# A fused block of four layers: factors' weights on two queues, condition's products behind the first flips, held gathers, and a further order of the pieces in steps 2 to 10

## The chip, the core and the metric

The kernel runs on one core of one Trainium2 chip. Its metric is the device time of one execution in microseconds (us). Before the change three executions took 637.67 us in the median (636.52 to 637.96).

## What is computed

The input x has 8 sequences of 256 tokens with 256 channels in fp32. Four layers follow one another, each added to its input: a conditioned attention with a gated MLP, a masked attention whose result is normed and modulated by the condition, a quaternion rotation, and a mixture of 8 experts of which each token takes two.

```python
# L0: conditioned norm, attention (16 heads of 16), gated MLP
g, b = t @ gw.T + gb, t @ bw.T + bb
xn = g * x * rsqrt(mean(x * x) + EPS) + b
x = x + attention(xn(x), Wq, Wk, Wv, Wo)
x = x + (silu(xn(x) @ gate_w.T) * (xn(x) @ hid_w.T)) @ out_w.T
# L1: masked attention, norm, modulation by the condition
out = softmax(where(mask, -inf, q @ k.T * scale)) @ v @ Wo.T
mod = silu(conditioning) @ Wc.T + bc
shift, sc = split(mod, 2)
xn = out / rms(out) * rms_scale * (1 + sc) + shift
# L2: a filter and two quaternion products, linear in x
x_rotated = hamilton(q_left_n, hamilton(x_filtered, q_right_conj))
# L3: router, two of eight experts
gate = (rms_w * norm(x)) @ wg_W + wg_b + (genre_embed @ gg_W + gg_b)
topk_w, topk_i = top_k(softmax(gate), 2)
h1 = relu(x @ W1 + b1); h2 = relu(h1 @ W2 + b2)
out = sum over the two experts of (h2 @ W3 + b3) * topk_w
```

## The kernel before

The eight sequences (number b, two blocks of 128 tokens each) go through the first three layers one behind another and overlap: while TensorE does the MLP of sequence b, the attention of a later one and the second attention of an earlier one are put in between. The order of TensorE, VectorE and ScalarE is the order of the program's text, and the text is driven by hand-written strings of words, `STEPS`, one string for each step. A word takes one piece of a generator: `S` is the scores of the next attention round with its exponential (`scores`, lines L1072 and L1074, or L1115 and L1120 for the second attention, named `LastKeys`), `O` its products with the values and the division (`values` and `divide`, L1085 or L1131 and L1096 to L1104), `W` the outward projection (L1144 or L1302), `p` and `q` the next piece of the projections and MLPs (`others`), `.n1` and `.n2` pieces of a norm, `.r1`, `.r2`, `.rot` and `.last` pieces of the second attention's norm and of the rotation with the router, `.pl` and `.table` pieces that place each token's choices in a table in memory, `.early`, `.e` and `.sure` pieces that set up and run expert tiles whose number is already certain.

Per sequence, `qkv_last` forms the keys, the router's part and the values of the second attention in one bank, `pkvl`: L1027 (16 matmuls of 32 x 64), L1034 (8 of 32 x 64) and L1041 (8 of 32 x 128). In the trace each fp32 matmul shows as two records. Then `project` (L982) makes the queries, `pq_a`.

At the start the first sequence is loaded in halves on SyncE's and ScalarE's queues (L581), `small_in` on ScalarE's (L565), the weights of the norms' factors `aff_w` in two halves on SyncE's (L621), the condition's weights `WcT` on GpSimd's (L565). TensorE multiplies the identity with itself meanwhile (`keep_busy`, L2031, written `unread`). Then come the factors (`paff`, L677), the condition's product (`pmod`, L776), the flips of the first normed sequence (`pt_n`, L964), the condition's product with the router's weights (L778, in the same bank) and the first keys (`pk_a`, L982). VectorE and ScalarE turn the flips into `xT_n` (L974, L972) with the factors `aff`.

The experts are worked in tiles of up to 256 tokens. `experts` runs a list of tiles: `records` reads the tile's entries of the table (L1641, SyncE), `fetch` its expert's weights of 2.18 MB (L1650, SyncE), `gather` its tokens by indirect DMA, 128 at a time, issued by GpSimd (L1659), `flip` transposes them (L1678), `hidden` (L1697) and `give` (L1733, L1749) do the layers and add the result to the output. The early tile runs inside steps 8 and 9, four sure tiles from step 9 on, then the rest. `AHEAD` is 3: of the sure tiles, the first three are gathered before the first is flipped. The order of GpSimd's and SyncE's instructions from step 2 on is the scheduler's, by dependences and text.

In the step texts `.sure` stands once near the end of step 8 and twice in step 9. The first `.sure` before the change reads the records and gathers tiles 0, 1 and 2 (six indirect DMAs):

```python
        for i in range(1, AHEAD + 1):
            if groups == NG:
                up_to(i, "fetch", fetch)
            up_to(i, "gather", gather)
        yield
        up_to(AHEAD, "fetch", fetch)
        yield
        flip(0)
        yield
```

Of the kernel before, what the change touches and what calls it, by code (L numbers as in the profile page):

```python
# [18 lines left out]
C = 64  # L19
# [52 lines left out]

STEPS = {
    2: (
        "p*5 .n1 p .n1 p S O p S W p O .n1 S p O p .n2 W p .n2*2 S .pl .r1*3 p*2 S .r1 p .rot*4 p .rot*3 "
        "p end p*3"
    ),
    3: (
        "O S .n1 p*3 W p .last S O p*2 .last .n1 .n2 S p W .r1 p*2 .r1 p .n1 p S .r1 .pl .n2 p .r1 .rot "
        "p .last O S .last .n2 p*3 .rot*2 end .rot p .rot*2 p*2 .rot p"  # L80
    ),
    4: (
        ".last p O S p .last p W .last p S O .n1 p*2 .n2 .n1 p W .last*3 p .n1 p S .pl .n2 .r1 p*2 .pl "
        ".r1 S .r1 .pl p*2 .r1 .pl p .pl*2 p .pl*2 p .rot p .rot .n2 .rot S .rot .pl O .rot p .rot p*2 "
        ".rot end"
    ),
    5: (
        ".n1*2 .last O .last S p*2 S O .last*2 p*2 .pl W p W .r1 p .r1 p .r1*2 S p*2 O .n2 .rot .n2 "
        ".rot*2 S p .n2 .n1 p S .rot p*6 .rot p .rot*2 p*2 end"
    ),  # L90
    6: (
        "O S p O W .last p*2 S .last .n2 .last*2 p*2 S .last p .last W .n2 .pl*3 .n2 p*3 .early .r1*2 "
        "p*2 .pl .early p .pl .r1 .pl .r1 .pl*2 p S .pl O p .early q p S .rot*6 end p*2 .rot"
    ),
# [5 lines left out]
    ),  # L100
    9: ".r2*4 .sure .last S .sure p O .last p*2 .last*3 W .last*2 p*2",
    10: ".r1*2 p .r1*2 p .rot*7 p .rot p*3 .rot p .rot*4 p*3 .rot .pl*6 p .rot*2 .pl*3",
}


# [428 lines left out]
def block_kernel(ctx: ExitStack, tc: tile.TileContext, a: dict, out: bass.AP):  # L534
# [82 lines left out]
    ggw, wgb_b, ggb_b = part["ggw"][0:C, :], part["wgb"], part["ggb"]  # L617
    aff_w = work.tile([C, 4, D], F32, tag="pe", bufs=3, name="aff_w")
    first_factors, second_factors = slice(0, 2), slice(2, 4)
    for js in (first_factors, second_factors):  # L620
        nc.sync.dma_start(out=aff_w[:, js, :], in_=a["aff_w"][:, js, :])  # L621
    wk0 = load_w(nc.sync, "L0_WkT", D, D, pool_a)
    wq0 = load_w(nc.sync, "L0_WqT", D, D, pool_a)
    xs_in[1] = load_x(1)
# [144 lines left out]
    def set_up_condition(cond_g):  # L769

        all3 = ps_s.tile([P, 4 * 2 * S], F32, tag="s", name="pmod")[:, 0 : 2 * KC * 32 + B * E]
        pm = all3[:, 0 : 2 * KC * 32].rearrange("p (k d) -> p k d", d=32)
        pg = all3[:, 2 * KC * 32 :]
        quarters = wcT.rearrange("c (k i d) -> c i k d", k=2 * KC, i=4)
        for i in range(4):
            nc.tensor.matmul(pm[32 * i : 32 * i + 32], silu_c, quarters[:, i], start=True, stop=True)  # L776
        yield
        nc.tensor.matmul(pg, ones[0:C, :], cond_g.rearrange("c b e -> c (b e)"), start=True, stop=True)  # L778
# [208 lines left out]
    def qkv(xT, wq, wk, wv, name):  # L987
# [22 lines left out]
        yield  # L1010
        return qz, kT, va

    def qkv_last(xT, b, xg):

        n = len(va_bufs["a1"])
# [22 lines left out]
        for k in range(KC):  # L1038
            for i in range(0, P, 32):
                c, at = divmod(i, KS)  # L1040
                nc.tensor.matmul(  # L1041
                    pv[i : i + 32, :], near[:, k, at : at + 32], wv1[:, k, c * P : (c + 1) * P],
                    start=k == 0, stop=k == KC - 1,
                )
# [577 lines left out]
    def smaller(size, n):  # L1622
        return f"p{size}_{n}", lambda what: todos["parts"][0:1, what, size, n : n + 1], *PIECES[size]

    def experts(items, pl, key, groups=NG, near_end=None):

        st = [{} for _ in items]
# [26 lines left out]
        def gather(n):  # L1654
            _, _, nq, p = items[n]
            rec = st[n]["rec"]
            xg = pl.tile("xg", [P, MOST, D], f"xg_{name_of(n)}")
            for q in range(nq):
                nc.gpsimd.indirect_dma_start(  # L1659
                    out=xg[0:p, q, :], out_offset=None, in_=tokens[0 : reach(n), :],  # L1660
                    in_offset=bass.IndirectOffsetOnAxis(ap=rec[0:p, q, 0:1], axis=0),
                )
            st[n]["xg"] = xg

        def flip(n):
# [367 lines left out]
    by_text = {mybir.EngineType.DVE, mybir.EngineType.Activation, mybir.EngineType.Pool}  # L2033
    with tc.manual_schedule(engines=by_text):
        unread = ps_o.tile([P, P], F32, tag="o", name="unread")
        keep_busy(9)
        n1 = first_norm(0)
        next(n1)
        condition = set_up_condition(prepare_condition())
        next(n1)  # L2040
        factors = set_up_factors()
        next(factors)
        next(condition)
        do(n1)
        do(factors)
        g0 = first(0)
# [295 lines left out]
```

## Time and profile before

| what | us |
|---|---|
| median of three runs (lowest, highest) | 637.67 (636.52, 637.96) |
| the profiled execution, its own time | 638.67 |
| its span, first to last instruction | 636.8 |
| TensorE busy in the span | 617.9 |
| VectorE, ScalarE, GpSimd busy | 352.8, 207.6, 166.7 |
| mean granted clock of TensorE | 0.992 |

The profile is of one execution, which took 1.00 us more than the median of the three runs. Times in the views are from the span's start. A matmul's end is modelled, so a busy TensorE is not TensorE at its peak; a gap in its timeline, though, is time in which no matmul began. "issue" as the end of a gap means that the engine waited for nothing the profile shows. The granted clock is 1.00 at full speed and 0.50 at half.

### The profile page before, as it was taken

How to read it: one execution, taken by the hardware profiler on the slowest of the kernel's cores; microseconds unless marked ns; L12 is line 12 of the kernel's file. 1: busy time of each engine (PE TensorE's matmuls, PEld its weight loads, DVE VectorE, ACT ScalarE, POOL GpSimd, SP SyncE). 2: the span in 40 equal slices, each digit the busy share in tenths (PEclk: the TensorE clock that was granted, in tenths of full speed). 3: DMA queues.
4: the chain of work that ended last, by engine and by line, in shares of the span. 5: the costliest groups of instructions: out<-in, count | busy, mean ns of one | idle time of the engine just before them, and what ended most of it. 6: DMA issues, size and time to landing. Idle time of an engine off the chain costs nothing.

```text
span 636.8 us, 11270 instructions
## 1 busy us (share of the span) xinstructions
PE 617.9 (97%) x4320; PEld 491.8 (77%) x4320; DVE 352.8 (55%) x1126; ACT 207.6 (33%) x384; POOL 166.7 (26%) x292
## 2 busy tenths in 40 slices
PE   7999999999999999999999979999999999999995
PEld 6557787677778777768687856888888898989994
DVE  5664535876776975688788838993222222222221
ACT  3763323544335334352433213212121211212221
POOL 7701200000000530004201451256534343334113
PEclk8999999999999999999999999999999999999999
DMA  8711200100121110011015027743786567668512
GB/s 286 211 34 51 42 2 9 49 3 18 42 69 24 36 10 17 19 49 19 2 39 202 2 52 295 227 146 52 213 295 197 164 214 253 196 184 292 179 20 32
DMA packets 28624, 67.58 MB, mean 106 GB/s; under 512 B 8992, under 2 KB 22112, under 8 KB 26256
## 3 DMA queue, kind: packets, MB, share of 16 engines
q1 hardware_dynamic: 19776, 55.47, 26.3%
q0 software_dynamic: 8496, 11.11, 8.4%
q8 instruction: 36, 0.59, 0.4%
q14 instruction: 28, 0.23, 0.1%
q10 hardware_dynamic: 288, 0.18, 0.1%
HBM read 57.31 MB, written 9.44 MB: 105 GB/s over the span
## 4 chain that ended last, share of the span: by engine, by line
PE 91%; DVE 4%; ACT 2%; issue 1%; DMA 0%; POOL 0%; POOLq 0%; DVEq 0%; ACTq 0%
PE ph_a_rest L1697 10%; PE ph_a_p L1697 9%; PE ph L1252 9%; PE pg L1252 9%; PE pd L1265 8%; PE s_a L1072 5%; PE pq_a L982 5%; PE ph_s_sure L1697 4%; PE o_a L1085 4%; PE pe_a_p L1733 3%; PE pe_a_rest L1733 3%; PE py L1144 2%; PE py L1302 2%; PE pk_a L982 2%; PE pv_a L1006 2%; PE pe_s_sure L1733 2%
## 5 line engine op out<-in xcount | busy, mean ns | idle before, releaser
L1074 ACT ACTIVATE pe_a<-s_a 128x2048 f32<-128x2048 f32 x32 | 60.0, 1876 | 66.1 <-PE s_a L1072 65.4
L1252 PE MATMUL pg<-xT_n,gate_wT 128*128 128x256 f32 x256 | 61.4, 383 | 0.1
L1252 PE MATMUL ph<-xT_n,hid_wT 128*128 128x256 f32 x256 | 61.4, 383 | 0.0
L1265 PE MATMUL pd<-out_wT,hT 128*128 128x256 f32 x256 | 59.8, 383 | 0.0
L1265 PEld LDWEIGHTS pd<-out_wT,hT 128*128 128x128 f32 x256 | 47.6, 190 | 12.1 <-issue 6.1
L1252 PEld LDWEIGHTS ph<-xT_n,hid_wT 128*128 128x128 f32 x256 | 47.7, 190 | 10.7 <-issue 2.3
L1252 PEld LDWEIGHTS pg<-xT_n,gate_wT 128*128 128x128 f32 x256 | 47.8, 190 | 10.0 <-issue 2.0
L1197 POOL TENSOR_SCALAR xT_n<-xr,aff 128x256 f32<-128x256 f32 x10 | 5.8, 589 | 173.5 <-DVE xr L1192 82.0
L1697 PE MATMUL ph_a_rest<-h_a_rest,w_a_rest 128*128 128x256 f32 x192 | 42.5, 380 | 0.0
L1697 PE MATMUL ph_a_p<-h_a_p,w_a_p 128*128 128x192 f32 (+3 forms) x224 | 40.2, 338 | 0.0
L1708 DVE TENSOR_SCALAR h_a_rest<-ph_a_rest,w_a_rest 128x256 f32<-128x256 f32 x24 | 11.6, 484 | 50.7 <-PE ph_a_rest L1697 48.5
L1697 PEld LDWEIGHTS ph_a_rest<-h_a_rest,w_a_rest 128*128 128x128 f32 x192 | 36.0, 190 | 4.6
L1697 PEld LDWEIGHTS ph_a_p<-h_a_p,w_a_p 128*128 128x128 f32 x224 | 37.2, 190 | 1.6
L1256 ACT ACTIVATE th<-pg 128x512 f32<-128x512 f32 x32 | 19.0, 595 | 57.3 <-PE pg L1252 57.1
L1072 PE MATMUL s_a<-qz_a,kT_a 32*128 32x512 f32 x256 | 36.5, 640 | 0.5
L1455 POOL DMA_INDIRECT slots<-rec,posi x32 | 32.7, 1022 | 10.2 <-issue 5.0
L1096 DVE STREAM_TRANSPOSE tu_a<-o_a 128x512 f32<-128x512 f32 x32 | 22.6, 705 | 22.9 <-PE o_a L1085 11.5
L1708 DVE TENSOR_SCALAR h_a_p<-ph_a_p,w_a_p 128x192 f32<-128x192 f32 (+3 forms) x28 | 12.1, 432 | 40.3 <-PE ph_a_p L1697 38.0
L1258 DVE SCALAR_TENSOR_TENSOR sg<-th,pg 128x512 f32<-128x512 f32 x32 | 21.8, 682 | 22.5 <-ACT th L1256 22.4
L1749 POOL DMA_INDIRECT out<-ye_a_p,trec_a_p x14 | 20.6, 1472 | 44.5 <-ACT ye_a_p L1747 27.9
L1085 PE MATMUL o_a<-pe_a,va 128*32 128x256 f32 x512 | 30.9, 382 | 0.0
L1697 PE MATMUL ph_s_sure<-h_s_sure,w_s_sure 128*128 128x256 f32 x128 | 28.8, 382 | 0.1
(391 smaller groups left out, 1144.1 us busy)
## 6 DMA issues: line engine op xcount, KB each, us to landing
w_a_p<-in_experts SPq DMA_DIRECT2D x7, 2180.0 KB, 9.1
w_a_rest<-in_experts SPq DMA_DIRECT2D x6, 2180.0 KB, 9.2
w_s_sure<-in_experts SPq DMA_DIRECT2D x4, 2180.0 KB, 11.7
w_s_early<-in_experts SPq DMA_DIRECT2D x1, 2180.0 KB
mod<-mod_rows SPq DMA_DIRECT2D x8, 256.0 KB, 3.3
tokens<-x SPq DMA_DIRECT2D x4, 512.0 KB, 3.0
out<-x SPq DMA_DIRECT2D x4, 512.0 KB, 4.1
x<-in_x SPq DMA_DIRECT2D x7, 256.0 KB, 3.5
```

Source lines behind the costliest of these rows:

```text
L982: nc.tensor.matmul(pp[:, c, :], w[:, k, c * P : (c + 1) * P], xT[:, k, :], start=k == 0, stop=k == KC - 1)
L1072: nc.tensor.matmul(sc[:, j], kT[r, c, kc * P : (kc + 1) * P], qz[r, c], start=True, stop=True)
L1074: nc.scalar.activation(pe, sc, AF.Exp)
L1085: nc.tensor.matmul(o[32 * i : 32 * i + 32, qd, :], va[:, kc, 8 * c + 4 * qd + i].rearrange("p a d -> p (a d)"), pe[:, 2 * qd + i // 2, i % ...
L1096: nc.vector.transpose(turned.rearrange("p q j a d -> p (q j a d)"), o.rearrange("p q s -> p (q s)"))
L1252: nc.tensor.matmul(ps[:, j, :], w[:, k, o : o + P], yT[:, k, :], start=k == 0, stop=k == KC - 1)
L1258: nc.vector.scalar_tensor_tensor(sg, th, 1.0, pg, ALU.add, ALU.mult)
L1265: nc.tensor.matmul(pd[:, t, :], hT[:, c, t * P : (t + 1) * P], out_w[:, c, :], start=c == 0, stop=c == HID // P - 1)
L1455: sc = nc.gpsimd.indirect_dma_start(out=slots, out_offset=bass.IndirectOffsetOnAxis(ap=posi[:, t : t + 1], axis=0), in_=rec, in_offset=None,)
L1697: nc.tensor.matmul(phs[c - c0][:, 0:many], w[:, o : o + P], src[:, k, 0:many], start=k == 0, stop=k == n_in - 1,)
L1708: relu = nc.vector.tensor_scalar(dst, src_, bias, 0.0, ALU.add, ALU.max)
L1733: mm = nc.tensor.matmul(pos[q][0:p, q % NQ2, :], h2[:, k, q * p : (q + 1) * p], w[:, o : o + D], start=k == 0, stop=k == MC - 1,)
```

## The change

- `aff_w`: the second half is loaded by ScalarE's queue instead of SyncE's.
- `WcT`: its load is issued by GpSimd behind the mask's two loads and the fill of `ones`.
- `keep_busy(9)` becomes `keep_busy(10)`; `keep_busy(2)` stands behind the factors, where the condition's `pmod` stood.
- `set_up_condition`: the router's product comes first and `pmod` second, both behind the first flips.
- `qkv_last` notes its last matmul in `valued`; `experts` gathers only tile 0 of the sure tiles at the first piece, and tiles 1 and 2 at the second, behind a wait for the last noted matmul (`behind_values`).
- `STEPS` 2 to 10 take the pieces in another order.

```diff
@@ STEPS
     2: (
-        "p*5 .n1 p .n1 p S O p S W p O .n1 S p O p .n2 W p .n2*2 S .pl .r1*3 p*2 S .r1 p .rot*4 p .rot*3 "
-        "p end p*3"
+        "p*3 S .n1 p .n1 O S p W p*4 S .n2 O .n1 .n2 p*2 O p W .n2 .pl .r1 S .r1*2 p*2 S .r1 p .rot*3 p "
+        ".rot p .rot*3 p*3 end"
     ),
     3: (
-        "O S .n1 p*3 W p .last S O p*2 .last .n1 .n2 S p W .r1 p*2 .r1 p .n1 p S .r1 .pl .n2 p .r1 .rot "
-        "p .last O S .last .n2 p*3 .rot*2 end .rot p .rot*2 p*2 .rot p"
+        "O S p*2 .n1 p S O p*2 .last .n1 S p*2 S W p W .r1 .last p*2 .r1 .pl .n1 .r1*2 p .n2 .rot .last "
+        "p*2 .n2 p O .n2 .rot S .rot p .last p .rot end p*2 .rot p .rot*2 p"
     ),
...
-    7: "p S O p W",
+    7: "p O S p W",
     8: (
-        ".n2 O p*3 .early*2 W .n2 .early p .e .early .e .r1 p .r1*2 .n2 .r1 .rot*2 .early p*3 .rot p*2 "
-        ".rot*3 q p q .rot*2 p*2 .rot*2 q end S .rot*2 .e .rot q*2 e .pl .rot .pl*2 q .pl*2 .table .pl e "
-        ".pl .table*3 q*2 .pl .table e q*2 .sure O q*4 W q*7 .pl"
+        "O .n2 p*2 .early .n2 p W .early p .e .early .e .r1 p*2 .r1 .early .n2 .r1*2 .rot*2 p*2 .early p "
+        ".rot p .rot*3 q p q .rot*2 p*2 .rot*2 q end S .rot .e .rot*3 q*2 e .pl*4 q e .pl .table .pl "
+        ".table .pl q .table*2 q .pl .table q*2 e O .sure q*4 W q*6 .pl q"
     ),
-    9: ".r2*4 .sure .last S .sure p O .last p*2 .last*3 W .last*2 p*2",
-    10: ".r1*2 p .r1*2 p .rot*7 p .rot p*3 .rot p .rot*4 p*3 .rot .pl*6 p .rot*2 .pl*3",
+    9: ".r2*2 S .sure .r2*2 .sure .last p .last O .last p*2 .last*3 W p .last p",
+    10: ".r1*2 p .r1*2 p .rot*8 p*4 .rot*2 p .rot*3 p*3 .pl*3 .rot .pl p .pl*3 .rot*2 .pl*2",
@@ block_kernel
-    for js in (first_factors, second_factors):
-        nc.sync.dma_start(out=aff_w[:, js, :], in_=a["aff_w"][:, js, :])
+    for eng, js in ((nc.sync, first_factors), (nc.scalar, second_factors)):
+        eng.dma_start(out=aff_w[:, js, :], in_=a["aff_w"][:, js, :])
...
-    wcT = load(nc.gpsimd, a["WcT"], [C, 2 * D], "WcT", pool=pool_b)
     lastT8 = pool_b.tile([P, 1], U8, tag="lastT8", bufs=1, name="lastT8")
     for c in range(KC):
         nc.gpsimd.dma_start(out=lastT8[c * KS : (c + 1) * KS, :], in_=a["maskT"][S - KS : S, 0:1])
     ones = const.tile([P, P], F32, tag="ones", name="ones")
     nc.gpsimd.memset(ones, 1.0)
+    wcT = load(nc.gpsimd, a["WcT"], [C, 2 * D], "WcT", pool=pool_b)
@@ set_up_condition
+        nc.tensor.matmul(pg, ones[0:C, :], cond_g.rearrange("c b e -> c (b e)"), start=True, stop=True)
         for i in range(4):
             nc.tensor.matmul(pm[32 * i : 32 * i + 32], silu_c, quarters[:, i], start=True, stop=True)
-        yield
-        nc.tensor.matmul(pg, ones[0:C, :], cond_g.rearrange("c b e -> c (b e)"), start=True, stop=True)
         yield
@@ qkv_last
+    valued = []
...
-                nc.tensor.matmul(
+                mm = nc.tensor.matmul(
                     pv[i : i + 32, :], near[:, k, at : at + 32], wv1[:, k, c * P : (c + 1) * P],
                     start=k == 0, stop=k == KC - 1,
                 )
+        valued.append(mm.ins)
@@ experts
+    def behind_values(ins):
+        assert len(valued) == B
+        tc.add_manual_dep(
+            ins, valued[-1].name, mybir.DependencyInfo(mybir.DependencyClass.Sync, mybir.DependencyReason.DATA),
+            reason="gathers behind the last keys and values",
+        )
...
-                nc.gpsimd.indirect_dma_start(
+                taken = nc.gpsimd.indirect_dma_start(
                     out=xg[0:p, q, :], out_offset=None, in_=tokens[0 : reach(n), :],
                     in_offset=bass.IndirectOffsetOnAxis(ap=rec[0:p, q, 0:1], axis=0),
                 )
+                if groups == NG - 1 and 0 < n < AHEAD:
+                    behind_values(taken.ins)
...
-            up_to(i, "gather", gather)
+            if groups != NG - 1:
+                up_to(i, "gather", gather)
+        if groups == NG - 1:
+            up_to(1, "gather", gather)
         yield
         up_to(AHEAD, "fetch", fetch)
+        up_to(AHEAD, "gather", gather)
         yield
@@ the start
-        keep_busy(9)
+        keep_busy(10)
         n1 = first_norm(0)
         next(n1)
         condition = set_up_condition(prepare_condition())
         next(n1)
         factors = set_up_factors()
         next(factors)
-        next(condition)
+        keep_busy(2)
         do(n1)
         do(factors)
```

More of the change, by code (lines that the diff above doesn't have):

```diff
@@ L74 @@
     2: (
-        "p*5 .n1 p .n1 p S O p S W p O .n1 S p O p .n2 W p .n2*2 S .pl .r1*3 p*2 S .r1 p .rot*4 p .rot*3 "
-        "p end p*3"
-    ),
-    3: (
-        "O S .n1 p*3 W p .last S O p*2 .last .n1 .n2 S p W .r1 p*2 .r1 p .n1 p S .r1 .pl .n2 p .r1 .rot "
-        "p .last O S .last .n2 p*3 .rot*2 end .rot p .rot*2 p*2 .rot p"
-    ),
-    4: (
-        ".last p O S p .last p W .last p S O .n1 p*2 .n2 .n1 p W .last*3 p .n1 p S .pl .n2 .r1 p*2 .pl "
-        ".r1 S .r1 .pl p*2 .r1 .pl p .pl*2 p .pl*2 p .rot p .rot .n2 .rot S .rot .pl O .rot p .rot p*2 "
-        ".rot end"
-    ),
-    5: (
-        ".n1*2 .last O .last S p*2 S O .last*2 p*2 .pl W p W .r1 p .r1 p .r1*2 S p*2 O .n2 .rot .n2 "
-        ".rot*2 S p .n2 .n1 p S .rot p*6 .rot p .rot*2 p*2 end"
-    ),
-    6: (
-        "O S p O W .last p*2 S .last .n2 .last*2 p*2 S .last p .last W .n2 .pl*3 .n2 p*3 .early .r1*2 "
-        "p*2 .pl .early p .pl .r1 .pl .r1 .pl*2 p S .pl O p .early q p S .rot*6 end p*2 .rot"
+        "p*3 S .n1 p .n1 O S p W p*4 S .n2 O .n1 .n2 p*2 O p W .n2 .pl .r1 S .r1*2 p*2 S .r1 p .rot*3 p "
+        ".rot p .rot*3 p*3 end"
+    ),
+    3: (
+        "O S p*2 .n1 p S O p*2 .last .n1 S p*2 S W p W .r1 .last p*2 .r1 .pl .n1 .r1*2 p .n2 .rot .last "
+        "p*2 .n2 p O .n2 .rot S .rot p .last p .rot end p*2 .rot p .rot*2 p"
+    ),
+    4: (
+        "p .last O S p .last p W .last p S O .n1 p*2 .n2 .n1 p W p .last p .last*2 .n1 .n2 .r1 S p*2 "
+        ".pl*2 .r1 S .r1 .pl p*2 .r1 .pl p .pl*3 p .pl .n2 p .rot p .rot*3 S .rot*2 .pl O p*2 .rot end p"
+    ),
+    5: (
+        ".n1 .last*2 .n1 O S .last p .last .pl p S O p*2 W p*2 W .r1 S .r1*2 p*3 .n2 .r1 .rot*2 .n2 .rot "
+        "S p O .n2 p .n1 S p end p .rot p*4 .rot p*2 .rot*2 p"
+    ),
+    6: (
+        "O S p O .last W .last S .n2 p*2 .last*2 p*2 S .last p .last W .n2 .pl*3 p*3 .r1*2 p*2 .n2 "
+        ".early p .pl .r1 .early .pl .r1 .pl*3 p S .pl O p .rot q .rot p S .rot*2 end .rot*2 p*2 .rot "
+        ".early"
     ),
[1 row of a table removed]
[1 row of a table added]
     8: (
[3 rows of a table removed]
-    ),
-    9: ".r2*4 .sure .last S .sure p O .last p*2 .last*3 W .last*2 p*2",
-    10: ".r1*2 p .r1*2 p .rot*7 p .rot p*3 .rot p .rot*4 p*3 .rot .pl*6 p .rot*2 .pl*3",
[3 rows of a table added]
+    ),
+    9: ".r2*2 S .sure .r2*2 .sure .last p .last O .last p*2 .last*3 W p .last p",
+    10: ".r1*2 p .r1*2 p .rot*8 p*4 .rot*2 p .rot*3 p*3 .pl*3 .rot .pl p .pl*3 .rot*2 .pl*2",
 }
```

## The prediction

> **What bounds the kernel now.** I read the page's busy times and chain first, then TensorE's timeline over the whole span for its gaps, then the other engines' timelines and the granted clock at the two places where the gaps gather. TensorE is the bound nearly everywhere:
>
> ```profile
> PE 617.9 (97%) x4320; PEld 491.8 (77%) x4320; DVE 352.8 (55%) x1126; ACT 207.6 (33%) x384; POOL 166.7 (26%) x292
> PE 91%; DVE 4%; ACT 2%; issue 1%; DMA 0%; POOL 0%; POOLq 0%; DVEq 0%; ACTq 0%
> ```
>
> TensorE is 97% busy, and the chain lies 91% on it. Behind the head (to 10.2 us) and before the last scatters its gaps sum to 6.70 us: 0.65 before 83.62, 0.39 before 220.52, 0.86 before 307.07, 0.40 before 343.88, 1.20 before 373.64, six inside the last sequence's keys and values (2.18), 0.68 before 385.72, 0.34 before 394.62. From 88 to 220 there is none. From 395 to 627 VectorE and the loads cost TensorE no gap either. Thus a gain won before 395 reaches the end, and little is to be won outside these places.
>
> The largest place is `pkvl`. First an undisturbed one, then the one at 342.48 with the two gathers of the early tile beside it, then the last:
>
> ```profile
> 130.19 0.65 PE L1027 MATMUL pkvl<-x2T,L_WkT 128*32 128x64 f32 x32
> 130.66 0.41 PE L1034 MATMUL pkvl<-x2T,gcols 128*32 128x64 f32 x16
> 130.89 0.62 PE L1041 MATMUL pkvl<-wv,x2T 128*32 128x128 f32 x16
> 131.44 0.66 PE L938 MATMUL pt_n<-ident,xs_n 128*128 128x128 f32 x4
> ...
> 343.88 0.67 PE L1041 MATMUL pkvl<-wv,x2T 128*32 128x128 f32 x15 [0.40 <-issue]
> ...
> 376.07 0.65 PE L1027 MATMUL pkvl<-x2T,L_WkT 128*32 128x64 f32 x32
> 376.54 0.54 PE L1034 MATMUL pkvl<-x2T,gcols 128*32 128x64 f32 x13
> 377.51 0.31 PE L1034 MATMUL pkvl<-x2T,gcols 128*32 128x64 f32 x3 [0.43 <-issue]
> 378.23 0.43 PE L1041 MATMUL pkvl<-wv,x2T 128*32 128x128 f32 x4 [0.41 <-issue]
> ...
> 381.12 0.61 PE L1041 MATMUL pkvl<-wv,x2T 128*32 128x128 f32 x2 [0.45 <-issue]
> 381.67 3.38 PE L982 MATMUL pq_a<-x2T,L_WqT 128*128 128x256 f32 x8
> 385.72 1.12 PE L1115 MATMUL s_a<-qT_a,kz_a 32*64 32x256 f32 x32 [0.68 <-ACT qT_a L1056]
> ```
>
> Undisturbed it takes 131.44 - 130.19 = 1.25 us, the last time 381.67 - 376.07 = 5.60. In its gaps TensorE waits for nothing the profile shows. GpSimd's timeline has the likely cause:
>
> ```profile
> 372.42 0.99 POOL L1659 DMA_INDIRECT xg_s_sure<-tokens,trec_s_sure  x1 [3.69 <-DMA trec_s_sure<-slots]
> 373.72 1.44 POOL L1659 DMA_INDIRECT xg_s_sure<-tokens,trec_s_sure  x1 [0.30 <-issue]
> ...
> 379.24 0.96 POOL L1659 DMA_INDIRECT xg_s_sure<-tokens,trec_s_sure  x1 [0.30 <-issue]
> ```
>
> Six gathers run from 372.42 to 380.20, and the gaps end 1.5 us later. The `pkvl` at 219.28 has four scatters of step 4 around it and one gap (0.39), the one at 342.48 two gathers and one gap (0.40); those at 85.52, 130.19, 174.67, 264.94 and 307.07 have no indirect DMA beside them and no gap. The granted clock adds to it:
>
> ```profile
> 380.00:381.00 1.00, 0.37 (x3) 0.00 (x0) 0.00 (x0) 0.00 (x0) 0.20 (x1) 1.00 0.24 78
> 382.00:383.00 1.00, 1.00 (x3) 0.82 (x3) 0.97 (x6) 0.00 (x0) 0.00 (x0) 0.50 0.00 0
> ```
>
> The clock (the third number from the right) falls to 0.50 at 381.1, until 384.5, so `pq_a` takes 3.38 us where it took 1.89 at 131.93.
>
> The head is a second place:
>
> ```profile
> 7.46 0.64 PE L677 MATMUL paff<-aff_w,small_in 64*32 64x256 f32 x8 [1.76 <-DMA aff_w<-in_aff_w]
> 7.89 0.42 PE L776 MATMUL pmod<-WcT,silu_c 64*32 64x128 f32 x8
> 8.76 0.89 PE L964 MATMUL pt_n<-ident,xs_n 128*128 128x128 f32 x4 [0.44 <-ACT xs_n L950]
> 9.57 0.69 PE L778 MATMUL pmod<-cond_g,ones 64*128 64x64 f32 x2
> 10.19 3.09 PE L982 MATMUL pk_a<-xT_n,L_WkT 128*128 128x256 f32 x8
> ```
>
> The factors wait 1.76 us for their weights, but the chain does not go through them: it goes load of x (to 3.76), VectorE's norm to 8.17, `xs_n` to 8.71, the flips, and `xT_n`, which ScalarE ends at 10.24, and `pk_a` starts then. `aff` is ready at 9.34, before the first `xT_n` at 9.45. `pk_a` takes 3.09 us instead of 1.89: the clock is 0.50 from 9.05 to 12.4.
>
> **The change part by part.** *Held gathers.* The two gathers of tile 0 stay at 372.42, as their entries arrive then. The other four (1.26 us apart) wait for the last matmul of `pkvl`; behind that wait in GpSimd's queue stand only tile 3's gathers, which wait for the first flips anyway. Price for `pkvl`: 5.60 falls to 1.25 plus one gap of 0.40, as with two gathers at 342.48, so -3.95. Bounds: no gap at all, -4.35; gaps of the old kind for about half the time, -2.2. With TensorE busy again the clock stays up: `pq_a` from 3.38 to 1.89, -1.49 (bounds 0 and -1.49). The four gathers then run from about 378 to 383; tile 1 is flipped at 403.11 and tile 2 at 419.08, so even with 5.5 us taken from those times some 15 us cover them. Without that cover a tile would wait up to the 5 us that the four take.
>
> Given back: `pq_a` is 1.49 faster, VectorE's work behind `pkvl` is not. From the end of `pkvl` VectorE needs, in step 9's new order, 4.69 (values to `x3`, 381.77 to 386.46), then 0.6 copy of the flips, two rotation pieces of 0.6, a relu of 0.4, the shift of `wo` 0.3 and both divisions 4.0, that is 11.2 us to the second `oT`. TensorE's own way to there is 1.82 + 0.66 + 1.05 + 0.50 + 1.82 + 1.02 + 3.56 + 0.5 = 10.9. So the wait before L1302 stays about 0.3 to 0.5, against 0.34: +0.1, at most +0.9 if both rotation pieces wait for the exponential round. The 0.68 for `qT_a` stays, as nothing stands between. Sum: -3.95 - 1.49 + 0.1 = -5.3.
>
> [...] The rows above show the gaps; which way they come about, no row shows, and if it isn't the gathers this part is worth 0, the first rival below.
>
> *The head.* SyncE issues one load fewer (two took 1.19), so `WkT` and what follows leave it 0.6 us earlier. ScalarE issues one more (0.45 as `small_in`, up to 0.59) ahead of its table load (1.74 to 3.02), behind which it idles 0.52 for x: +0.1 on its first square at most, and VectorE's own half of the norm ends later. The second half of `aff_w` then lands 2.7 to 4.8 us after its issue at 1.7 (rows of `small_in` and `aff_w`), by 6.5 instead of 7.4: worth 0, as `aff` is off the chain. `WcT` leaves GpSimd at about 3.0 instead of 1.62 (its 0.75 of issue is only exchanged with the mask's 1.11 and the fill's 0.26). Between 2.7 and 8.2 us (`small_in`, `gate_w`) it lands by 5.7 to 11.2; I take 8.5 with `aff_w`'s 5.5, before `pmod` wants it at 9.6. The extra `unread` (0.47 each) and the two behind the factors lie in the 1.76 + 0.44 idle: 0, if they end before 8.71. `pmod` is put between the flips and `pk_a`: 0.42, up to 0.84 at half clock; the router's product (0.69) ends with `xT_n` as now, so `pmod` is on the path. At half clock +0.4; nearer 0 if its four parts overlap; +1.7 if `WcT` lands at 11.2. The busy share of TensorE before 9.05 changes little (0.6 us more unread work, 0.42 less), so I take the clock's fall as given: +0.4. If it stays up, `pt_n` and `pk_a` save 0.3 + 1.2.
>
> [...]
>
> *The order of steps 2 to 10.* The number of matmuls is the same. Of the gaps that an order could close, 0.86 (`x2T` behind an exponential), 1.20 (`x2` behind two divisions) and 0.68 have the same instructions in the same order around them; 0.39 and 0.40 come with indirect DMAs that stay. On the other side the new texts put attention rounds earlier. Step 2 has the scores at the third instead of the seventh MLP product; then the exponential (1.88), two squares (1.05) and the norm's chain of nine (1.77) stand before the division: 1.07 + 0.1 + 1.88 + 1.05 + 1.77 + 1.9 = 7.8 us to `oT`, where TensorE needs 1.07 + 1.9 + 1.86 + 1.1 + 1.9 = 7.8 to reach `W`. Just covered. In step 7 the exponential gets `W` between it and its use. I take 0, bounds -1 and +3 (three such chains late by 1 us each).
>
> Sum: -5.3 + 0.4 + 0 = -4.9. On the profiled execution's own time 638.67 this gives 633.8; its span would be 631.9. That execution lies 1.0 above the median, so for the median I predict 637.67 - 4.9 = 632.8.
>
> **The rivals.** *The stall follows the gathers.* Put behind `pkvl`, the four gathers meet L1115 (32 matmuls in 1.05 us, 33 ns each) and L1131, as dense as L1041 (34 ns each), in which most gaps stood. For it: the gathers are as many. Against it: L1131 at 389.09 runs its 32 matmuls in 1.09 us with tile 3's gathers (387.70 to 389.92) and the weights' loads beside it. If two thirds of 4.35 and half the clock's price return, 632.8 + 2.9 + 0.7 = 636.4; if the gaps weren't the gathers' doing, 637.67 + 0.4 = 638.1.
>
> *The clock stays up at the head.* The better filled 5.7 to 8.7 us would do it: 632.8 - 1.5 - 0.4 = 630.9. Against it: still 1.7 us idle before the flips.
>
> *Slower: the exponential ends last in the rounds brought forward.* Steps 2 to 6 each have such a round. If ScalarE's squares or VectorE's chain of nine then stand before each division by one exponential (1.88) too much, `W` waits 1.88 in each: 5 x 1.88 = 9.4 against 4.9, so 637.67 + 4.5 = 642.2; slower from the third such step on. For it: each engine works in the text's order, and the old text had no gap from 88 to 220. Against it: step 2's sum above just closes, and in steps 6 and 7 the scores gain distance.
>
> **How the numbers follow.** Forecast 0.62 (its own range 631.5 to 635.5), stall follows 0.18, clock up 0.10, slower order 0.10. Two executions of before lie 0.2% apart, so about 1.3 us is what a measurement can tell from no change. Faster (below 636.4): 0.62 + 0.10 + half of 0.18 = 0.81. Within: 0.10, the other half and a little of the slow order. Slower: 0.09. The range that leaves out 2 in 10 reaches from 630.5 (clock up) to 637.0 (the stall mostly back).
>
> **What would show it.** Four of six gathers after the last record of L1041, and `pkvl` of the last sequence in 1.3 to 2.1 us; clock 1.00 there and `pq_a` under 2 us; no new gaps at L1115 and L1131; a wait before the last L1302 under 0.6. At the head `paff` by 6.5, `pk_a` still at 10.2 to 10.7. No gap over 0.5 us between 88 and 370 but the known ones. Wrong would be: gaps in `pkvl` without gathers beside them, or the saved time back in waits for VectorE before 420.

## The result and the profile after

The changed kernel took 635.89 us in the median of 22 executions (631.95 to 637.97), the kernel before 637.20 on the same chip (635.24 to 639.82): a ratio of 0.9971, 95% interval 0.9957 to 0.9985. It is faster, by 0.3% where 0.76% was forecast. On a second chip the ratio was 0.9956 (0.9930 to 0.9981).

The profiled execution after took 636.67 us, with a span of 634.9 (before 638.67 and 636.8). Its page, first the busy times, then the shares of the chain of work that ended last:

```profile
PE 617.2 (97%) x4326; PEld 491.4 (77%) x4326; DVE 353.6 (56%) x1126; ACT 207.5 (33%) x384; POOL 167.7 (26%) x292
PE 92%; DVE 3%; ACT 3%; issue 1%; POOL 0%; ACTq 0%; POOLq 0%
```

TensorE is still the bound, so the difference has to be read in its gaps and its clock. The largest place of before, the last `pkvl` and what follows, in TensorE's timeline of the kernel after:

```profile
378.20 0.65 PE L1028 MATMUL pkvl<-x2T,L_WkT 128*32 128x64 f32 x32
378.67 0.41 PE L1035 MATMUL pkvl<-x2T,gcols 128*32 128x64 f32 x16
378.89 0.62 PE L1042 MATMUL pkvl<-wv,x2T 128*32 128x128 f32 x16
379.44 1.99 PE L981 MATMUL pq_a<-x2T,L_WqT 128*128 128x256 f32 x8
382.11 1.12 PE L1117 MATMUL s_a<-qT_a,kz_a 32*64 32x256 f32 x32 [0.68 <-ACT qT_a L1058]
383.17 0.66 PE L1689 MATMUL ptx_s_sure<-ident,xg_s_sure 128*128 128x128 f32 x4
383.66 1.89 PE L1708 MATMUL ph_s_early<-h_s_early,w_s_early 128*128 128x256 f32 x8
387.50 1.10 PE L1133 MATMUL o_a<-pe_a,vl 64*32 64x256 f32 x32 [1.95 <-ACT pe_a L1122]
...
394.23 3.07 PE L1744 MATMUL pe_s_early<-w_s_early,h_s_early 128*128 128x256 f32 x13
```

`pkvl` takes 1.24 us without a gap (5.60 before) and `pq_a` 1.99 (3.38 before). New is the wait of 1.95 us before `o_a`, for an exponential that began late. The other engines' timelines in that stretch of the same kernel show how:

```profile
383.59 0.95 POOL L1668 DMA_INDIRECT xg_s_sure<-tokens,trec_s_sure  x1 [0.30 <-issue]
385.87 0.95 POOL L1668 DMA_INDIRECT xg_s_sure<-tokens,trec_s_sure  x1 [1.32 <-PE ph_s_early L1708]
...
385.57 1.88 ACT L1122 ACTIVATE pe_a<-s_a 128x2048 f32<-128x2048 f32 x1 [3.51 <-PE ph_s_early L1708]
...
385.63 0.69 DVE L1693 COPY xt_s_sure<-ptx_s_sure 128x512 f32<-128x512 f32 x1 [1.24 <-PE ph_s_early L1708]
```

The scores `s_a` end at 383.23 and the flips `ptx_s_sure` at 383.83. Yet ScalarE starts the exponential at 385.57, VectorE the copy of the flips at 385.63 and GpSimd the gather that needs their buffer at 385.87: all three at the end of `ph_s_early` (385.55), which none of them reads. TensorE's completion signals for `s_a` and `ptx_s_sure` reached the others 2.3 and 1.8 us after the products. The trace's record of the semaphore that TensorE raises says the same: it was raised at 385.55, 385.61 and 385.70 for products that ended at 383.24, 383.83 and 385.55, while for `pkvl` and `pq_a` it was raised within 0.05 us of the product's end. Before, the same exponential began 0.1 us after its scores, which ended at 386.84:

```profile
386.94 1.88 ACT L1120 ACTIVATE pe_a<-s_a 128x2048 f32<-128x2048 f32 x1 [1.28 <-PE s_a L1115]
```

The start in TensorE's timeline of the kernel after:

```profile
6.04 0.64 PE L677 MATMUL paff<-aff_w,small_in 64*32 64x256 f32 x8 [0.40 <-DMA aff_w<-in_aff_w]
6.61 0.71 PE L2046 MATMUL unread<-ident 128*128 128x128 f32 x4
8.84 1.12 PE L963 MATMUL pt_n<-ident,xs_n 128*128 128x128 f32 x4 [1.52 <-ACT xs_n L949]
...
11.09 3.78 PE L981 MATMUL pk_a<-xT_n,L_WkT 128*128 128x256 f32 x8
14.66 2.18 PE L981 MATMUL pq_a<-xT_n,L_WqT 128*128 128x256 f32 x8
16.67 1.89 PE L1005 MATMUL pv_a<-L_WvT,xT_n 128*128 128x256 f32 x8
```

And two windows of the same kernel (the third number from the right is the granted clock):

```profile
8.00:12.00 4.00, 3.16 (x16) 2.24 (x17) 3.08 (x14) 1.98 (x6) 0.88 (x17) 0.55 1.06 383
12.00:16.00 4.00, 4.00 (x12) 3.20 (x12) 1.92 (x12) 1.10 (x3) 3.23 (x7) 0.60 1.03 394
```

The factors' weights land 1.4 us sooner in this profile (0.1 and 0.4 us sooner in `again` and `g_py` below, which have the same start), but the flips `pt_n` still wait for `xs_n`, now for 1.52 us, and the clock stands at 0.50 from 8.40 to 15.23 (before: 9.04 to 12.45). The first values' products `pv_a` come at 16.67; before they came at 14.85.

Added up over the two profiles, with the start of each stretch on TensorE as the mark:

| stretch | before | after | difference |
|---|---|---|---|
| start to the first `pv_a` | 14.85 | 16.67 | +1.82 |
| to the last `pkvl` | 361.22 | 361.53 | +0.31 |
| to the last `s_a` | 9.65 | 3.91 | -5.74 |
| to the last `o_a` | 3.37 | 5.39 | +2.02 |
| to `pe_s_early` | 7.01 | 6.73 | -0.28 |
| to the end of the span | 240.75 | 240.70 | -0.05 |

The sum is -1.92. So the gain asked for was there, -5.74, and in these two executions two thirds of it went elsewhere: 2.02 into a new wait, 1.82 into the start.

### The profile page after: what moved, and what is told of

Its sections match the earlier page's. It is cut to its first block, busy times and chain, and to the rows that moved or that the text cites. A ratio compares the mean times of both kernels' runs of the same rounds, so it can differ in the third digit from the quotient of the medians.

```text
span 634.9 us, 11285 instructions
## 1 busy us (share of the span) xinstructions
PE 617.2 (97%) x4326; PEld 491.4 (77%) x4326; DVE 353.6 (56%) x1126; ACT 207.5 (33%) x384; POOL 167.7 (26%) x292
## 4 chain that ended last, share of the span: by engine, by line
PE 92%; DVE 3%; ACT 3%; issue 1%; POOL 0%; ACTq 0%; POOLq 0%
PE ph_a_rest L1708 10%; PE ph_a_p L1708 9%; PE ph L1254 9%; PE pg L1254 9%; PE pd L1267 8%; PE ph_s_sure L1708 6%; PE s_a L1074 5%; PE pq_a L981 5%; PE o_a L1087 4%; PE pe_a_p L1744 3%; PE pe_a_rest L1744 3%; PE pk_a L981 2%; PE py L1304 2%; PE py L1146 2%; PE pe_s_sure L1744 2%; PE pv_a L1005 2%
## 6 DMA issues: line engine op xcount, KB each, us to landing
w_a_rest<-in_experts SPq DMA_DIRECT2D x6, 2180.0 KB, 10.2
```

## The experiments

Kernels that stand together below shared one chip and its executions of the kernel before; ratios are to those, with 95% intervals. The chips differ (before: 642.62, 637.01 and 639.47 us in the three groups), so times are compared within a group.

**First group: which part does what.** Theory A: the wait before `o_a` comes with the held gathers; its rival puts it down to the step texts. Theory B: the loss at the start is a matter of when the clock falls; its rival takes it for a fixed price.

`held` is the kernel before with the held gathers alone:

```diff
+        valued.append(mm.ins)
...
+                if groups == NG - 1 and 0 < n < AHEAD:
+                    behind_values(taken.ins)
...
         up_to(AHEAD, "fetch", fetch)
+        up_to(AHEAD, "gather", gather)
```

> The held gathers alone, all else as before. Theory A (the gathers cost the last pkvl and the clock, 5.8 us, and about 2 us come back as a wait for the exponential of the last round): 3.5 to 4.0 us faster than before, ratio 0.994; pkvl of the last sequence in 1.25 us, pq_a in 1.9 us, a wait of about 2 us before L1131. Theory B (the new step texts make the wait for the exponential, the held gathers do not): 5.5 us faster, ratio 0.991, no wait over 0.5 us before L1131. Theory C (the stall is there in some executions only): within 2 us of before.

Measured 638.64 us, ratio 0.9938 (0.9920 to 0.9957). TensorE's timeline:

```profile
379.46 0.65 PE L1029 MATMUL pkvl<-x2T,L_WkT 128*32 128x64 f32 x32
379.94 0.41 PE L1036 MATMUL pkvl<-x2T,gcols 128*32 128x64 f32 x16
380.16 0.62 PE L1043 MATMUL pkvl<-wv,x2T 128*32 128x128 f32 x16
...
388.90 1.10 PE L1134 MATMUL o_a<-pe_a,vl 64*32 64x256 f32 x32 [2.08 <-ACT pe_a L1123]
```

No gap in the last `pkvl`, 3.92 us from it to `s_a`, and a wait of 2.08 before `o_a`, with the old step texts: theory A.

`head` is the kernel before with the new start alone:

```diff
-    for js in (first_factors, second_factors):
-        nc.sync.dma_start(out=aff_w[:, js, :], in_=a["aff_w"][:, js, :])
+    for eng, js in ((nc.sync, first_factors), (nc.scalar, second_factors)):
+        eng.dma_start(out=aff_w[:, js, :], in_=a["aff_w"][:, js, :])
...
-        keep_busy(9)
+        keep_busy(10)
...
-        next(condition)
+        keep_busy(2)
```

> The start alone (factors' weights on two queues, the condition's weights behind, its products behind the flips, ten and two unread products). Theory A (the condition's product lies between flips and keys at half clock, and the clock comes back later): 1 to 2 us slower than before, ratio 1.002 to 1.003, first keys from 11.0 us. [...]

Measured 640.93 us, ratio 0.9985 (0.9956 to 1.0015), no difference that shows. But its executions spread from 636.56 to 644.7, and its profile has a short start: the first keys at 9.15, where theory A had 11.0, the clock at full speed (1.00 in the windows from 8 to 20 us, `pk_a` in 1.99), `pv_a` at 12.71. The same start that cost 1.8 us in one profile gains 2.1 in another.

`order` is the kernel before with the new step texts alone:

```diff
-    7: "p S O p W",
+    7: "p O S p W",
...
```

> The step texts alone. Theory A (the order is worth nothing by itself): within 1 us of before, the last pkvl with its gaps (over 4 us), no new gap over 0.5 us from 88 to 370. Theory B (the order loses): 1 to 3 us slower, with new waits in steps 2 to 6 or in step 9.

Measured 641.0 us, ratio 0.9978 (0.9963 to 0.9993): a little gained, which neither theory expected. Its profile has the old gaps in `pkvl` (0.45, 0.43, 1.02, 0.33 us), behind which the clock was at half for 10.2 us from 381.1 (mean 0.57 between 380 and 392, `pq_a` in 3.78), so the profile itself is longer than that of before.

`nohead` is the changed kernel with the old start:

```diff
-    for eng, js in ((nc.sync, first_factors), (nc.scalar, second_factors)):
-        eng.dma_start(out=aff_w[:, js, :], in_=a["aff_w"][:, js, :])
+    for js in (first_factors, second_factors):
+        nc.sync.dma_start(out=aff_w[:, js, :], in_=a["aff_w"][:, js, :])
...
```

> Held gathers and step texts with the start as before, that is the changed kernel less its start. Theory A: 1 to 2 us faster than the changed kernel, 3.5 to 4 us faster than before, ratio 0.994. [...]

Measured 637.3 us, ratio 0.9917 (0.9891 to 0.9943), a wait of 2.05 before `o_a`. On this chip gathers and texts together gain what was forecast for them (-5.3 of 637.67 is 0.9917), in spite of that wait and more than theory A's 0.994; on the next chip they do not.

**Second group: what makes the signals late, and what the start costs.** `again` is the changed kernel itself:

> The changed kernel once more, unaltered, as the measure for the three kernels beside it. If the start costs nothing (theory B: the head's loss is a matter of when the clock falls), its ratio to the kernel before is that of the kernel with the old start beside it, within 0.2%; if the start costs what the changed kernel's first trace shows (1.83 us at the first values' products), it is 0.3% above that one.

Measured 636.21 us, ratio 0.9956 (0.9930 to 0.9981).

`nohead2` is `nohead` once more:

> Held gathers and step order with the old start, once more, beside the changed kernel on one chip. Theory B (the start is worth nothing either way): the two ratios agree within 0.2%. Rival (the start costs 1.8 us): this one is 0.3% below the changed kernel.

Measured 635.42 us, ratio 0.9969 (0.9947 to 0.9991): no difference to `again` that these intervals show, in favour of theory B: in the median the new start costs and gains nothing that can be told. The ratio of one and the same kernel moved from 0.9917 to 0.9969 between two chips, so comparisons across the groups are no finer than half a per cent.

`g_late` puts the held gathers behind the last exponential:

```diff
-            nc.scalar.activation(self.pe, sc, AF.Exp)
+            exped.append(nc.scalar.activation(self.pe, sc, AF.Exp).ins)
...
-            ins, valued[-1].name,
+            ins, exped[-1].name,
```

> The changed kernel with the held gathers put behind the last round's exponential and no longer behind the last key and value products. In the changed kernel's trace that exponential began 2.33 us after the last score product and TensorE waited 1.95 us before o_a. Theory G (TensorE's completion signals are late because GpSimd issues gathers beside it): the exponential begins within 0.2 us of the end of the scores, the wait before o_a falls from 1.95 us to under 0.3, and the time falls by some 1.5 to 2 us (0.3%). Theory W (the experts' weights, 2,180 KB a tile, which set out 3.6 us sooner, delay the signals): exponential and wait stay as in the changed kernel, about 2.3 and 1.95 us. Rival to both (the delay belongs to the dense row of small products themselves): no change either.

Measured 637.62 us, ratio 0.9977 (0.9948 to 1.0005): nothing gained in time. The timelines of ScalarE, TensorE and VectorE, one behind the other, say why ("remote" stands where the trace names no releaser):

```profile
378.56 1.88 ACT L1122 ACTIVATE pe_a<-s_a 128x2048 f32<-128x2048 f32 x1 [1.28 <-PE s_a L1117]
...
380.70 1.09 PE L1133 MATMUL o_a<-pe_a,vl 64*32 64x256 f32 x32
...
386.31 0.68 PE L1304 MATMUL py<-wo,oT_a 128*128 128x264 f32 x2 [0.87 <-DVE oT_a L1106]
388.26 3.01 PE L1304 MATMUL py<-wo,oT_a 128*128 128x264 f32 x6 [1.26 <-DVE low L2199]
...
384.22 0.72 DVE L1098 STREAM_TRANSPOSE tu_a<-o_a 128x512 f32<-128x512 f32 x1 [2.25 <-remote]
...
389.28 0.48 DVE L1719 TENSOR_SCALAR h_s_early<-ph_s_early,w_s_early 128x256 f32<-128x256 f32 x1 [0.50 <-remote]
```

The scores ended at 378.45; the exponential begins at 378.56 and `o_a` without a wait. But now the gathers run from 380.70 to 387.97, and VectorE's division of `o_a`, whose products end at 381.79, begins at 384.22, 2.4 us late. The late signal has moved with the gathers, to the next product beside them. It does not stop at small products: the 16 large matmuls of `ph_s_early` behind `o_a` end at 385.44, their signal is recorded at 389.25, and VectorE, idle for 0.50 us before it, begins to read them at 389.28. TensorE did not wait for that one. The clock was at half from 387.93 to 391.34 besides, behind the first wait for `oT_a` (the six records of `py` from 388.26 took 3.01 us, eight took 2.24 in `g_py`).

`w_late` leaves the gathers and holds the first fetch of the experts' weights instead:

```diff
+            if groups == NG - 1 and n == 0:
+                behind_exponential(asked_for.ins)
```

> The changed kernel with the first fetch of the late sure tiles' weights (w_s_sure, which set out at 381.65 us) put behind the last round's exponential; the gathers as in the changed kernel. Theory W: the exponential begins within 0.2 us of the end of the scores, and the wait of 1.95 us before o_a goes, 1.5 to 2 us off the time. Theory G: the wait stays at about 1.95 us and the time within 0.2% of the changed kernel's.

Measured 636.95 us, ratio 0.9975 (0.9950 to 1.0000). ScalarE's and TensorE's timelines:

```profile
384.91 1.88 ACT L1122 ACTIVATE pe_a<-s_a 128x2048 f32<-128x2048 f32 x1 [3.47 <-remote]
...
386.84 1.10 PE L1133 MATMUL o_a<-pe_a,vl 64*32 64x256 f32 x32 [1.91 <-ACT pe_a L1122]
```

The weights set out at 386.92, after the exponential, and the wait is unchanged: the weights are not the cause.

**Third group: both losses undone.** Among the first ten profiles VectorE's second or first small step of the first norm (`rq_v`, `rq_y`) was 1.8 to 2.1 us long in eight and 0.17 in two, `head` and `g_late`, which were the two with the short start. In the kernel after, VectorE and GpSimd stand so:

```profile
4.59 2.08 DVE L657 TENSOR_SCALAR rq_v_n<-ss_n 128x2 f32<-128x2 f32 x1
...
4.81 1.84 POOL L748 MEMSET va<- 128x1024 f32 x2
```

The step on 128 x 2 numbers ends as GpSimd's two memsets of 128 x 1024 do (6.67 and 6.65). In `head` the memset began at 5.49, since `small_in` had landed later, and the step took 0.17. `ones` is the changed kernel with the memsets moved behind those steps:

```diff
+        for va in va_bufs["a0"]:
+            ones_of = nc.gpsimd.memset(va, 1.0)
+            tc.add_manual_dep(
+                ones_of.ins, halved[0].name, ...
+                reason="ones behind the first norm's one-operand steps",
```

> The changed kernel with GpSimd's two memsets of the values' ones (va, 1.84 us) put behind the second step of the first norm's reciprocal root on VectorE. In the profiles so far VectorE's first steps rq_v or rq_y took 1.97 to 2.08 us where they met that memset (xs_n at 8.16 to 8.28 us, first values' products pv_a at 16.6 to 16.7), and 0.17 us where the memset came after them (xs_n at 6.58 to 6.60, clock 1.00, pv_a at 12.3 to 12.7). Theory S (that meeting, decided by which load lands first, makes the two lengths of the start): rq_v and rq_y take 0.17 us, xs_n begins by 6.7 us, pv_a by 13.5 us in the profile, the clock does not fall in the first 16 us, and the median falls by 2 to 3 us below the changed kernel's (ratio to before about 0.993). Rival (the landing of aff_w, which TensorE awaited for 0.4 to 1.25 us, or the clock by itself decides): xs_n is early all the same, but pv_a stays at 16 us or later and the median within 1 us of the changed kernel's.

Measured 635.77 us, ratio 0.9946 (0.9921 to 0.9971). Its start, on TensorE, VectorE and GpSimd:

```profile
7.72 0.60 PE L974 MATMUL pt_n<-ident,xs_n 128*128 128x128 f32 x4
...
9.16 1.99 PE L992 MATMUL pk_a<-xT_n,L_WkT 128*128 128x256 f32 x8
10.99 1.89 PE L992 MATMUL pq_a<-xT_n,L_WqT 128*128 128x256 f32 x8
12.72 1.89 PE L1016 MATMUL pv_a<-L_WvT,xT_n 128*128 128x256 f32 x8
...
4.64 0.17 DVE L659 TENSOR_SCALAR rq_v_n<-ss_n 128x2 f32<-128x2 f32 x1
...
5.12 1.84 POOL L756 MEMSET va<- 128x1024 f32 x2
```

`pv_a` comes 3.95 us sooner than in the kernel after, at full clock. The time falls by less than forecast: beside the changed kernel's 0.9971 and 0.9956 on other chips, 0.9946 is no clear gain, and its nine executions still spread over 5.1 us (633.61 to 638.75). In this profile the wait before `o_a` (the gathers lie as in the kernel after) was followed by 3.4 us at half clock from 385.08, and `pe_s_early` came 8.05 us after `o_a` instead of 6.73: the second loss was larger here.

`ones_b` is the kernel before with the same move of the memsets:

> The kernel before with the same memsets put behind the first norm's second step, nothing else. Theory S: xs_n at about 6.6 us (8.3 before), pv_a at 12.5 to 13.5 us (14.85 before) unless aff_w lands later than that leaves room for (7.46 us before: then pv_a at about 13.5 to 14.5), ratio 0.996 to 0.998. If the old start reaches what the new one does, the new start is worth nothing by itself; if it stays a microsecond or more behind, the factors' second queue is what the new start adds. Rival: as before, within 0.1%.

Measured 638.62 us, ratio 1.0004 (0.9987 to 1.0022). The step takes 0.17 here too, but `aff_w` on one queue lands at 6.99, TensorE waits 1.29 for it, the clock is at half from 9.02 to 12.43 (`pk_a` in 3.62 us instead of 1.99), and `pv_a` is at 14.29. The forecast ratio of 0.996 to 0.998 did not come. So in these profiles the old start does not use what the move gives, and the new one does.

`g_py` is the changed kernel with the held gathers behind the last round's output products, where TensorE goes on with large ones:

```diff
-            ins, valued[-1].name,
+            ins, turned_out[-1].name,
...
-        up_to(AHEAD, "gather", gather)
+        if groups != NG - 1:
+            up_to(AHEAD, "gather", gather)
```

> The changed kernel with the held gathers issued behind the last round's output products (py, which ended at 394.3 us in the changed kernel), where TensorE next runs only large products. Theory G (signals are late wherever gathers run beside rows of small products): the last exponential begins within 0.2 us of the scores' end, o_a waits under 0.3 us, its division begins within 0.2 us of its end, py within 5 us of o_a, and the stretch from the scores to pe_s_early, 12.12 us in the changed kernel and 13.73 with the gathers behind the exponential, shortens to about 10; the time falls by some 2 us (0.3%), provided tile 1's tokens land before its flip (401.2 in the changed kernel). Rival (late signals hit whatever large products run beside the gathers too): the stretch shortens as well, but TensorE waits 1 to 2 us between pe_s_early and the flip of tile 1, and nothing is gained at the end.

Measured 634.91 us, ratio 0.9929 (0.9901 to 0.9956). Its timelines, TensorE, ScalarE, VectorE and GpSimd in turn:

```profile
382.29 1.12 PE L1117 MATMUL s_a<-qT_a,kz_a 32*64 32x256 f32 x32 [0.68 <-ACT qT_a L1058]
...
385.65 1.09 PE L1133 MATMUL o_a<-pe_a,vl 64*32 64x256 f32 x32
...
392.35 3.72 PE L1745 MATMUL pe_s_early<-w_s_early,h_s_early 128*128 128x256 f32 x16
...
383.51 1.88 ACT L1122 ACTIVATE pe_a<-s_a 128x2048 f32<-128x2048 f32 x1 [1.28 <-PE s_a L1117]
...
386.84 0.72 DVE L1098 STREAM_TRANSPOSE tu_a<-o_a 128x512 f32<-128x512 f32 x1
...
392.75 1.07 POOL L1669 DMA_INDIRECT xg_s_sure<-tokens,trec_s_sure  x1 [15.29 <-PE py L1304]
```

The exponential starts 0.1 us after the scores, the division 0.1 after `o_a`, and `s_a` to `pe_s_early` takes 10.06 us (12.12 in the kernel after). The products are the same small ones with the same spacing, so it is not they alone that delay the signals. TensorE has no gap behind `pe_s_early` either. Alone, this kernel's interval still overlaps the changed kernel's.

Signals stay late in the record here too, but no reader waits for them. VectorE reads `pe_s_early` at 396.11, right at its end (396.07). The flips of tile 1, behind it, end at 399.96, and the signal recorded next comes at 402.69, 2.7 us later (0.02 us in the kernel after, where no gathers run beside these flips). Their copy on VectorE begins only at 405.60, behind other work.

`both` has the edits of `ones` and `g_py`:

> The changed kernel with both edits: memsets behind the first norm's second step, held gathers behind py. If both theories hold the gains add: 4 to 5 us below the changed kernel, ratio to before about 0.990. If one falls, the time is that of the other alone.

Measured 631.47 us (630.92 to 634.14), ratio 0.9888 (0.9863 to 0.9913): it beats both kernels, and its interval lies below both that the changed kernel gave (0.9957 to 0.9985, and 0.9930 to 0.9981). The changed kernel was not run on this chip, but the distance is more than the half per cent that chips differ by. TensorE's timeline:

```profile
12.52 1.89 PE L1016 MATMUL pv_a<-L_WvT,xT_n 128*128 128x256 f32 x8
...
388.69 3.72 PE L1756 MATMUL pe_s_early<-w_s_early,h_s_early 128*128 128x256 f32 x16
```

Its span is 629.7, 5.3 us below that of the kernel after: `pv_a` at 12.52 (-4.15), and from the last `pkvl` to `pe_s_early` 13.97 us instead of 16.03 (-2.06); some 0.9 goes back in the stretches between.

The stretch from the last `pkvl` on, in all the variants that tell the causes apart:

| kernel | gathers run beside | `pkvl` to `s_a` | `s_a` to `o_a` | `o_a` to `pe_s_early` | sum |
|---|---|---|---|---|---|
| before | `pkvl` | 9.65 | 3.37 | 7.01 | 20.03 |
| after | `s_a` | 3.91 | 5.39 | 6.73 | 16.03 |
| `w_late` | `s_a` | 3.92 | 5.34 | 6.77 | 16.03 |
| `g_late` | `o_a` | 3.91 | 3.37 | 10.36 | 17.64 |
| `g_py` | `pe_s_early` | 3.92 | 3.36 | 6.70 | 13.98 |

In each row the loss stands where the gathers stand, and beside `pe_s_early` there is none. In `g_late` part of the loss is the clock at half.

## Why the prediction was right in part

**The direction held, the size did not.** 635.89 lies in the wide range (630.5 to 637.0) and just outside the forecast's own (631.5 to 635.5). 4.9 us were forecast. The two profiles differ by 1.92, the medians by 1.3. By the table of stretches the 3.0 that lack in the profiles are 1.6 in the step "given back", 1.4 at the head and 0.3 in the order, less 0.3 by which `pkvl` was better than forecast.

**Held gathers, `pkvl` and `pq_a`: right.** Forecast -3.95 - 1.49 = -5.44, measured -5.74: there is not even the one gap that two gathers left at 342.48, as tile 0's two gathers end before `pkvl` begins. The cause, an inference from GpSimd's timeline, was shown by `held`: moving the gathers alone removes the gaps. (One reading was off: the last gap ended 0.9 us after the last gather, at 381.12; what came 1.5 us after it was `pq_a`.) The clock's share, 1.49, is not won in every execution: in `head` the gaps were there and the clock stayed up, with `pq_a` at 1.99.

**The step that failed: "Given back ... +0.1, at most +0.9".** Measured +2.02 - 0.28 = +1.74. That sum let each engine start when its input was computed. It looked for the wait before L1302 and rightly found it small (none in the kernel after); the wait came earlier, before `o_a` (L1131 before, L1133 after), because the exponential's start signal was late. The rival "the stall follows the gathers" was the nearer one: its 636.4 stands 0.5 from the median, 635.89, in part by luck, as the start had a share in the loss that this rival did not have. Its form was wrong too. It foresaw gaps among the products of L1115 and L1131, and those products run at their old spacing; late are the signals that they are done. Its counter-argument, that L1131 beside tile 3's gathers took 1.09 us, looked at the product and not at who waits for it: the division behind it began 0.40 us after its end.

A plainer sign stood in the profile of before. The exponential of an earlier sequence began 1.79 us after its scores ended (226.87), beside GpSimd's scatters, with ScalarE idle:

```profile
225.45 1.42 PE L1115 MATMUL s_a<-qT_a,kz_a 32*64 32x256 f32 x32
...
228.66 1.88 ACT L1120 ACTIVATE pe_a<-s_a 128x2048 f32<-128x2048 f32 x1 [3.44 <-remote]
```

No product on TensorE waited for it, so a search for TensorE's gaps passes it by. What shows this kind of loss is the distance between the end of a product and the start of the first instruction that reads it.

**The head: the sum fits no profile, as the start has several lengths.** "so I take the clock's fall as given: +0.4" failed too: it puts `pv_a` at 15.25, and none of the eight profiles with the new start has it there; the profile after shows +1.82. `pmod` did move onto the path as foreseen; most of the rest went with the clock, at half for 6.83 us instead of 3.41. In the four profiles with the new start and a long `rq_v` or `rq_y` (after, `again`, `w_late`, `g_py`) `pv_a` stood at 16.3 to 16.8; in the four with the short one (`head`, `g_late`, `ones`, `both`) at 12.3 to 12.7. The old start gave 14.3 to 16.7. The rival "the clock stays up at the head" thus came true in some executions. The changed kernel's 22 times spread over 6.0 us (the kernel before's over 4.6), while five of the six of `both` lie within 0.84; that fits a start of two lengths, and so do the six of `g_py`, one at 631.55 and five at 634.86 to 635.78. The nine of `ones` fit less well (over 5.1 us, with the memsets moved), and which start each timed execution had was not recorded.

A cause of the two lengths stood in the profile of before, in VectorE's and GpSimd's timelines:

```profile
4.78 1.81 DVE L657 TENSOR_SCALAR rq_v_n<-ss_n 128x2 f32<-128x2 f32 x1
...
4.72 1.84 POOL L748 MEMSET va<- 128x1024 f32 x2
```

`rq_v` took 1.81 us where its neighbours took 0.17, on the very chain that the prediction walked ("VectorE's norm to 8.17"), and its length was taken over without a question. Which steps were long beside the fill, the traces show: `rq_v` or `rq_y`, both `tensor_scalar`, ended with the memset (6.59 and 6.56 in the kernel before, 6.67 and 6.65 after), while the steps with two tensors ran on beside it at 0.16 us each in `ones`. Which came first, they show less well: in the kernel after `rq_v` stands from 4.59, the memset from 4.81, GpSimd's product before it from 4.61. What ties the two, no run shows.

The clock has its own share in the start's length. The stretches at half clock that ended inside the span lasted 3.41 us (before, two of them; `g_late`, `ones_b`), 6.83 (after) and 10.2 (`order`); what starts one, no run shows. In `again` and `w_late` TensorE ran slow from the factors on (`paff` took 1.08 us instead of 0.64, the `unread` products behind it 1.22 instead of 0.71), ahead of any effect of the memset. How much of the long starts is the clock's and how much the memset's was not told apart.

**The order of steps 2 to 10: forecast 0, bounds -1 and +3.** `order` gained 0.22% (0.07 to 0.37), some 1.4 us, a little past the lower bound; where, the profiles don't show, as the stretch from `pv_a` to the last `pkvl` is 0.31 us longer after than before. The rival "the exponential ends last in the rounds brought forward" fell: between 130 and 360 us the kernel after has four gaps, of 0.42, 0.31, 0.30 and 0.41 us, and only the 0.31 is a wait for an exponential, the late one at 230.50.

## What to carry to other kernels

Before moving indirect DMAs off one place, look at what runs at the next, and who waits for it. Here the gathers cost TensorE its pace (`pkvl` in 5.60 us instead of 1.24) or its readers their signals (1.8 to 2.5 us late) beside rows of small products; beside large ones a signal could be late too (2.7 and 3.8 us), but nothing that TensorE needed soon hung on it. So look for a place behind the small products where the readers have time to spare, and not merely one behind those that suffered. Check the distance from the end of a product to the start of its reader, not only the gaps on TensorE. When a VectorE step on a few numbers takes ten times its neighbours' time, look at what GpSimd does beside it: here it was a fill (1.81 to 2.08 us for the step against 0.17), and with the fill moved, a load that had been made earlier in vain became worth something (`pv_a` at 12.72 in `ones`, at 14.29 in `ones_b`).

## What the runs showed of the hardware that was not expected

- TensorE's completion signals came 1.8 to 2.5 us after the products, while the products themselves ran at full pace and clock. It happened with GpSimd's gathers beside rows of products that take 33 ns each (after, `again`, `held`, `nohead`, `w_late` at the exponential, `g_late` at the division) and not at those two products without gathers there (`g_py`, `both`). For larger products beside gathers signals were late as well, by 3.8 us (`ph_s_early` in `g_late`) and 2.7 us (flips of tile 1 in `g_py` and `both`), where TensorE waited for none of them. Earlier in the kernel, beside GpSimd's scatters, the same exponential of another sequence began 2.0 us late (at 230.50 us in the kernel after), and 1.8 in the kernel before. What lets the signals go was not found out: in the seven profiles with the long wait before `o_a` the exponential began within 0.15 us of the end of `ph_s_early`, and also 0.97 to 1.17 us after the last held gather, so these two are not told apart, and the division in `g_late` began with `ph_s_early` and the gathers still running. Nor was it found out how the gathers made TensorE's gaps in `pkvl`.
- A VectorE step on 128 x 2 numbers took 1.8 to 2.1 us instead of 0.17 beside GpSimd's fill of 1.84 us. With the clock, that went with more than 4 us at the start: `g_late` and `g_py` have the same program up to 370 us, and their first values' products stand at 12.31 and 16.78 us.
- Some gaps (0.42, 0.30 and 0.41 us) stay beside GpSimd's scatters and gathers at 222, 310 and 346 us in the kernel after. They were left alone.
